# Second-layer messages of a two-layer graph network added up in three tables by turns in place of four

## The chip, the cores and the metric

One core of one Trainium2 chip runs the whole kernel as one program. The time is the device time of one execution in microseconds (us). The engines named below: TensorE (PE, with its weight loads as PEld), VectorE (DVE), ScalarE (ACT), GpSimd (POOL), and SyncE (SP), which issues most of the transfers.

## The reference

Two message-passing layers over a graph with N = 12500 nodes of 160 numbers (64 scalars and 32 vectors of three) and E = 212500 edges, sorted by `dst`. The second layer, which the change touches, gathers by `dst` and sums by `src` (`edge_index` is `src, dst`; inside the layer the first is the one that is summed over):

```python
h = jnp.maximum(_layernorm(x, axis=-1), 0.0)
# second layer: s, v are linear maps of h; sh1 = unit vector of edge_attr_3 times sqrt(3)
w = jax.nn.relu(edge_feature @ W_fc1) @ W_fc2
xs = s[dst]
xv = v[dst]
out0a = w0 * xs
out0b = w3 * (jnp.einsum('emi,ei->em', xv, sh1) * INV_SQRT3)
out1a = (w1 * xs)[:, :, None] * sh1[:, None, :]
out1b = w2[:, :, None] * xv
out1c = w4[:, :, None] * (jnp.cross(xv, sh1[:, None, :]) * INV_SQRT2)
tp = jnp.concatenate([out0a, out0b, out1a.reshape(E, -1), out1b.reshape(E, -1), out1c.reshape(E, -1)], axis=-1)
agg = jax.ops.segment_sum(tp, src, num_segments=N) / DENOM
out_s = agg[:, :96] @ W_out_s + skip_s
out_v = jnp.einsum('nmi,mk->nki', agg[:, 96:].reshape(N, 128, 3), W_out_v) + skip_v
# a gate on out_s and out_v, and x + that is the output
```

So each edge gives a message of 480 numbers, and the messages of all edges with the same `src` are added into one row of a table with one row per node. The sum doesn't depend on how the edges are split over partial tables, up to rounding.

## The kernel before

Edges are padded to T = 1668 tiles of P = 128. Everything runs from one unrolled program, in stages.

**First layer** (lines 362 to 401). For each of 556 groups of three tiles, GpSimd gathers source rows with an indirect DMA per tile (line 367), and the sums are formed by matmuls and written by SP. In the same stage SP clears the tables of the second layer, three blocks of 128 rows at a time (`clear(acc1[k], C1, b0, 3)`, line 395, the DMA itself at line 185), once in four groups until all K tables of 99 blocks are cleared: 33 clears a table. VectorE also finds here, for every tile, which edge is the first with its `src`, and leaves in `where` the row to which each edge's sum goes: the first of equal edges gets the node's row, the others a trash row.

**Node stage** between the layers (lines 480 to 509): writes the gather table `ft1` and the skip term `skip`.

**Second layer** (lines 583 to 714). The loop runs over 417 groups `q` of G = 4 tiles. For each group VectorE builds `same` (which edges of a tile share a `src`, line 565) and the messages (`second_messages`, lines 535 to 560). `scattered` then handles each tile `j`: a matmul adds equal edges within the tile into `sm` in PSUM (line 671), ScalarE copies it to `o` in SBUF (line 673), and GpSimd issues an indirect DMA that adds the 128 rows of 480 floats (1920 bytes) to rows `where` of a table in HBM (line 675). The tile `o` has eight buffers (line 672), so a copy waits until the scatter eight tiles earlier has landed. Tile `t = q*G + j` goes to table `t % K`. Two scatters into one table may add into the same row, so the framework makes each wait until the previous one into its table has landed. POOL has nothing else to do in this stage. Every 12 tiles, SP loads the next inputs (`rows`, 384 KB; `ft`, 384 KB; `to` and `fw`, four each of 24 and 20 KB), one (`rows`) or two turns of 12 tiles ahead.

**Final stage** (lines 729 to 758). 49 turns over pairs of node blocks (FB = 2). `added` loads the two blocks from each of the K tables into `t` (named `sums`, line 738) and the skip term (line 740), and adds the tables on VectorE (lines 742 and 743); it is called one turn ahead of `mapped`, and `t` has four buffers. `mapped` transposes on TensorE (lines 408, 409), copies (411 on ScalarE, 412 on VectorE), multiplies (416, 417), and VectorE adds the skip term (line 754); `second_out` applies the gate (lines 719 to 724) and ScalarE's queue stores the result. VectorE's instructions are kept in the order in which the program writes them: both adds of the next pair, then for each block of this pair the copy of line 412 and the add of line 754, then the gate of the pair before.

Of the kernel before, what the change touches and what calls it, by code (L numbers as in the profile page):

```python
# [14 lines left out]
ALU = mybir.AluOpType  # L15
# [26 lines left out]
NCH = T // CT  # L42
CE = CT * P
CW = CT // S
K = 4
TR = NP
NT = NP + P
C0 = 385
# [6 lines left out]
def gnn_kernel(ctx: ExitStack, tc: tile.TileContext, a, out):  # L55
    nc = tc.nc
    tt = nc.vector.tensor_tensor
# [82 lines left out]
    for m in range(3):  # L140
        f0 = m * 96
        while f0 < (m + 1) * 96:
            k, p0 = divmod(f0, P)
# [36 lines left out]
    sums = [dram.tile([NT, 4 * HC], F32, name=f"sums_{k}") for k in range(2)]  # L180
    acc1 = [dram.tile([NT, C1], F32, name=f"acc1_{k}") for k in range(K)]
    skip = dram.tile([NP, 192], F32, name="skip")

    def clear(t, cols, b0=0, n=NT // P):
        nc.sync.dma_start(t.rearrange("(p b) c -> p b c", p=P)[:, b0:b0 + n, :],
                          zero[:, None, :cols].to_broadcast([P, n, cols]))
# [112 lines left out]
    def keep(i):  # L299
        tc.keep_in_program_order(i)  # L300
# [15 lines left out]
    with ExitStack() as st:  # L316
# [45 lines left out]
        for gr in range(NG):  # L362
# [30 lines left out]
            k, b0 = divmod(gr // CW * 3, NT // P)  # L393
            if gr % CW == 1 and k < K:
                clear(acc1[k], C1, b0, 3)
# [7 lines left out]
    def mapped(wk, ps, s, nv, wv, ws, v0=0, keep=lambda i: i):  # L403

        s0 = 0 if v0 else 3 * nv
        tp = ps.tile([P, 4, P], F32, name="tp")
        for m in range(3):
            nc.tensor.transpose(tp[:nv, m, :], s[:, v0 + m * nv:v0 + (m + 1) * nv], ident)
        nc.tensor.transpose(tp[:96, 3, :], s[:, s0:s0 + 96], ident)
        st = wk.tile([P, 4, P], F32, name="st")  # L410
        nc.scalar.copy(st[:nv, 0:3], tp[:nv, 0:3])
        keep(nc.vector.tensor_copy(st[:96, 3], tp[:96, 3]))
        n = 96 + ws.shape[1]
        y = ps.tile([P, n], F32, name="y")
        for m in range(3):
            nc.tensor.matmul(y[:, m * V1:(m + 1) * V1], st[:nv, m, :], wv, start=True, stop=True)
        nc.tensor.matmul(y[:, 96:n], st[:96, 3, :], ws, start=True, stop=True)
        return y
# [61 lines left out]
    with tc.tile_pool(name="nwk1", bufs=2) as wk, tc.tile_pool(name="nps1", bufs=2, space=PSUM) as ps:  # L480
        for c in range(NCB):
            rows = []
            for k in range(2):
                t = wk.tile([P, CB, 4 * HC], F32, name="rows", bufs=3)
# [99 lines left out]
    with ExitStack() as st:  # L584
# [84 lines left out]
        def scattered(q, j, same, msg):  # L669
# [5 lines left out]
            nc.gpsimd.indirect_dma_start(  # L675
                out=acc1[t % K][:, :], out_offset=bass.IndirectOffsetOnAxis(ap=where[:, t:t + 1], axis=0),
                in_=o, in_offset=None, compute_op=ALU.add)
# [17 lines left out]
        for q in range(NQ1):  # L695
            ch, k = divmod(q, CT // G)
# [19 lines left out]
    def second_out(wk, s, xs, n, keep=lambda i: i):  # L716

        sig = wk.tile([P, n, 96], F32, name="sig")
        nc.scalar.activation(sig, s[:, :, 96:192], AF.Sigmoid)
        keep(tt(s[:, :, 96:160], s[:, :, 96:160], sig[:, :, 0:64], ALU.mult))  # L720
        keep(tt(split(s[:, :, 0:96]), split(s[:, :, 0:96]), sig[:, :, None, 64:96].to_broadcast([P, n, 3, V1]), ALU.mult))
        y = wk.tile([P, n, D], F32, name="yo")
        keep(tt(y[:, :, :S0], xs[:, :, :S0], s[:, :, 96:160], ALU.add))
        keep(tt(planes(y[:, :, S0:]), planes(xs[:, :, S0:]), split(s[:, :, 0:96]), ALU.add))
        return y
# [3 lines left out]
    with tc.tile_pool(name="fwk", bufs=4) as wk, tc.tile_pool(name="fps", bufs=3, space=PSUM) as ps:  # L729
        def two(t, b0):  # L730
            return t[0:NP, :].rearrange("(p b) c -> p b c", b=NB)[:, b0:b0 + FB, :]

        def added(b0):
            if b0 >= NB:
                return
            t = wk.tile([P, K, FB, C1], F32, name="sums")
            for k in range(K):
                nc.sync.dma_start(t[:, k], two(acc1[k], b0))
            s = wk.tile([P, FB, 192], F32, name="s")
            nc.sync.dma_start(s, two(skip, b0))  # L740
            h = K // 2
            keep(tt(t[:, 0:h], t[:, 0:h], t[:, h:K], ALU.add))
            keep(tt(t[:, 0], t[:, 0], t[:, 1], ALU.add))
            return t, s


        ready, gated = added(0), None
        for b0 in range(0, NB + FB, FB):
            t, s = ready or (None, None)
            ready = added(b0 + FB)  # L750
            if t is not None:
                for b in range(FB):
                    y = mapped(wk, ps, t[:, 0, b, :], 128, o1_v, o1_s, 96, keep)
                    keep(tt(s[:, b, :], y, s[:, b, :], ALU.add))
            if gated:
                y = second_out(wk, gated[0], xr[:, gated[1]:gated[1] + FB, :], FB, keep)
                nc.scalar.dma_start(two(out, gated[1]), y)
            gated = (s, b0)
# [37 lines left out]
    with tc.If(flag > 0):  # L796
        with tc.tile_pool(name="gwk", bufs=1) as wk, tc.tile_pool(name="gps", bufs=1, space=PSUM) as ps:
# [14 lines left out]
            with tc.For_i(0, NQ) as q:  # L812
# [4 lines left out]
                for a_ in range(2):  # L817
# [4 lines left out]
                    for j in range(S):  # L822
                        t = a_ * S + j
# [43 lines left out]
            with tc.For_i(0, T // G) as q:  # L867
# [10 lines left out]
                for j in range(G):  # L878
                    h, c = divmod(j, 2)
# [67 lines left out]
```

## Time and profile before

| what | us |
|---|---|
| three runs | 6560.95, 6565.19 (median), 6582.53 |
| the profiled execution, its own time | 6562.27 |
| its span, first to last instruction | 6560.5 |
| first layer's gathers, first to last issue | 280.8 to 2425.8 |
| clears of the second layer's tables | 282.9 to 1108.5 |
| second layer's scatters, first to last issue | 2864.5 to 6160.7 |
| final stage, first load of a table to the last | 6167.1 to 6530.6 |
| busy: PE, DVE, POOL, ACT | 5848.0, 4708.9, 4260.3, 2430.5 |

Half of the time is the scatter loop of the second layer. Shares of busy time for the whole span mix stages with different limits (PE 89%, DVE 72%, POOL 65%), so each stage is looked at by itself: its steps, and what each engine waited for. In rows of groups the columns are line, engine, operation, what is written from what, count, then busy time and mean ns of one, then the engine's idle time just before and what ended most of it. In rows of the timeline they are start, duration, engine, line, operation, and in brackets the idle time before and its releaser. In rows of waits: engine, tile and line that waited, for what, total us, times, longest. In rows of windows: the stretch, its length, then busy time and count of each engine asked for, the granted clock of TensorE, the share of the DMA engines and GB/s.

### The profile page before, as it was taken

How to read it: one execution, taken by the hardware profiler on the slowest of the kernel's cores; microseconds unless marked ns; L12 is line 12 of the kernel's file. 1: busy time of each engine (PE TensorE's matmuls, PEld its weight loads, DVE VectorE, ACT ScalarE, POOL GpSimd, SP SyncE). 2: the span in 40 equal slices, each digit the busy share in tenths (PEclk: the TensorE clock that was granted, in tenths of full speed). 3: DMA queues.
4: the chain of work that ended last, by engine and by line, in shares of the span. 5: the costliest groups of instructions: out<-in, count | busy, mean ns of one | idle time of the engine just before them, and what ended most of it. 6: DMA issues, size and time to landing. Idle time of an engine off the chain costs nothing.

```text
span 6560.5 us, 87170 instructions
## 1 busy us (share of the span) xinstructions
PE 5848.0 (89%) x22974; PEld 3347.0 (51%) x22974; DVE 4708.9 (72%) x11396; ACT 2430.5 (37%) x7896; POOL 4260.3 (65%) x3346
## 2 busy tenths in 40 slices
PE   6899999999999988869999999999999999999676
PEld 4566656566666556634444444444444444444466
DVE  5587878777865547667777777777777777777566
ACT  2222222222222213334555555555555555555311
POOL 0277777777777760047787877777787777878400
PEclk9999999999999998879999999999999999999755
DMA  9687887554544347469999999999999999999987
GB/s 351 242 252 239 246 243 223 126 127 126 126 110 93 92 118 278 186 126 165 166 165 166 166 165 165 166 167 166 166 167 165 167 165 164 168 164 167 215 303 262
DMA packets 653194, 1186.35 MB, mean 181 GB/s; under 512 B 94385, under 2 KB 506225, under 8 KB 648978
## 3 DMA queue, kind: packets, MB, share of 16 engines
q0 software_dynamic: 320256, 546.78, 53.4%
q1 hardware_dynamic: 319954, 617.36, 29.2%
q10 hardware_dynamic: 12480, 16.56, 0.7%
q8 instruction: 185, 3.03, 0.2%
q14 instruction: 319, 2.61, 0.1%
HBM read 528.25 MB, written 652.09 MB: 180 GB/s over the span
## 4 chain that ended last, share of the span: by engine, by line


## 5 line engine op out<-in xcount | busy, mean ns | idle before, releaser
L675 POOL DMA_INDIRECT acc<-o,where x1668 | 2621.4, 1572 | 1114.1 <-ACT o L673 695.8
L367 POOL DMA_INDIRECT g<-ft,idx_src x1668 | 1637.7, 982 | 787.3 <-issue 683.6
L671 PE MATMUL sm<-msg,same 128*128 128x480 f32 x3336 | 1842.2, 635 | 58.6 <-ACT o L673 54.0
L673 ACT COPY o<-sm 128x480 f32<-128x480 f32 x1668 | 931.5, 558 | 1502.5 <-DMA acc<-o,where 1053.6
L339 PE MATMUL ag<-pr,fac 128*128 128x320 f32 x3336 | 1084.0, 462 | 100.3 <-DVE pr L288 98.6
L657 PEld LDWEIGHTS gs<-fw,pick 32*128 32x128 f32 x3336 | 484.0, 188 | 797.7 <-ACT xv L533 436.8
L657 PE MATMUL gs<-fw,pick 32*128 32x160 f32 x3336 | 691.1, 327 | 196.3 <-ACT xv L533 195.4
L565 DVE TENSOR_TENSOR same<-rows,wp 128x512 f32<-128x512 int16 x417 | 286.6, 687 | 745.5 <-ACT wp L666 570.3
L671 PEld LDWEIGHTS sm<-msg,same 128*128 128x128 f32 x3336 | 544.6, 196 | 450.9 <-issue 219.3
L339 PEld LDWEIGHTS ag<-pr,fac 128*128 128x128 f32 x3336 | 604.4, 194 | 309.4 <-DVE pr L288 112.3
L294 PE MATMUL wp<-w,hs 64*128 64x192 f32 x3336 | 701.5, 345 | 0.6 <-ACT hs L358 0.6
L287 DVE TENSOR_TENSOR pr<-wp,g 128x384 f32<-128x384 f32 x556 | 309.4, 556 | 516.1 <-DMA g<-ft,idx_src 430.2
L294 PEld LDWEIGHTS wp<-w,hs 64*128 64x128 f32 x3336 | 536.3, 190 | 254.8 <-issue 253.0
L342 ACT COPY so<-ag 128x161 f32<-128x161 f32 x556 | 164.4, 296 | 1269.0 <-PE ag L339 1269.0
L538 DVE TENSOR_TENSOR pp<-xv,wp 128x1152 f32<-128x1152 f32 x417 | 561.7, 1347 | 0.0
L640 PE MATMUL wp<-w,hs 64*128 64x224 f32 x3336 | 552.8, 409 | 0.0
L389 DVE SCALAR_TENSOR_TENSOR seen<-rows,srcf,before 128x128 f32<-128x128 int16 x1668 | 523.4, 347 | 1.5 <-DMA rows<-in_src_low 1.5
L640 PEld LDWEIGHTS wp<-w,hs 64*128 64x128 f32 x3336 | 257.9, 189 | 397.3 <-issue 397.1
L288 DVE TENSOR_TENSOR pr<-wp,g 128x576 f32<-128x576 f32 x556 | 415.5, 747 | 0.0
L538 DVE TENSOR_TENSOR msg<-wp,xv 128x768 f32<-128x768 f32 x417 | 399.4, 958 | 14.3
L538 DVE TENSOR_TENSOR msg<-msg,wp 128x768 f32<-128x768 f32 x417 | 397.9, 954 | 14.5
L374 DVE TENSOR_TENSOR fac<-hit,sh 128x384 f32<-128x384 bf16 x556 | 309.5, 557 | 66.9 <-PE ag L339 53.3
(146 smaller groups left out, 6335.4 us busy)
## 6 DMA issues: line engine op xcount, KB each, us to landing
rows<-in_src_low SPq DMA_DIRECT2D x278, 384.0 KB
acc<-zero SPq DMA_DIRECT2D x132, 720.0 KB
sums<-acc SPq DMA_DIRECT2D x196, 480.0 KB
sums<-zero SPq DMA_DIRECT2D x2, 31878.0 KB
rows<-sums SPq DMA_DIRECT2D x28, 2254.0 KB
ft<-in_ea SPq DMA_DIRECT2D x139, 384.0 KB
sums<-so SPq DMA_DIRECT2D x556, 80.5 KB
g<-ft,idx_src POOLq DMA_INDIRECT x1668
```

The costliest lines, as they stand in the source:

```text
L288: tt(o[:, :, :, S0:].rearrange("p t k (m u) -> p t k m u", m=3), w[:, :, :, None, S0:96].to_broadcast([P, n, 2, 3, V1]), split(g[:, :, S0: ...
L294: keep(nc.tensor.matmul(wp[:, j].rearrange("p (k u) -> p k u", k=2)[:, :, 0:96], hs[a_ * 64:(a_ + 1) * 64, j * P:(j + 1) * P], w0_2[a_ * 6 ...
L339: keep(nc.tensor.matmul(ag[:, 0:2 * HB], fac[:, j].rearrange("p m w -> p (m w)"), pr[:, j, :], start=j == 0, stop=j == S - 1))
L367: nc.gpsimd.indirect_dma_start(out=g[:, j, :], out_offset=None, in_=ft0[:, :], in_offset=bass.IndirectOffsetOnAxis(ap=idx["src"][:, t0 + j ...
L374: tt(fac, hit[:, :, None, :].to_broadcast([P, S, 4, W]), sh[:, t0:t0 + S, :, None].to_broadcast([P, S, 4, W]), ALU.mult)
L389: nc.vector.scalar_tensor_tensor(seen, hidden["rows"][:, u * P:(u + 1) * P], srcf[:, t0 + j:t0 + j + 1], before, op0=ALU.is_equal, op1=ALU ...
L538: keep(tt(*args))
L640: keep(nc.tensor.matmul(part["wp", q][:, 2 * h + c, :224], part["hs", q][h * 64:(h + 1) * 64, c * P:(c + 1) * P], w1_2[h * 64:(h + 1) * 64 ...
L657: keep(nc.tensor.matmul(gs[:, j - lo, :], part["pick", ch][u * W:(u + 1) * W, v, :], part["fw", ch][u * W:(u + 1) * W, :], start=True, sto ...
L671: keep(nc.tensor.matmul(sm, same[:, j, :], msg[:, j, S0:], start=True, stop=True))
L673: keep(nc.scalar.copy(o, sm))
L675: nc.gpsimd.indirect_dma_start(out=acc1[t % K][:, :], out_offset=bass.IndirectOffsetOnAxis(ap=where[:, t:t + 1], axis=0), in_=o, in_offset ...
```

## The change

The second layer's sums are kept in three tables, tile `t` going to table `t % 3`. One table fewer is cleared in the first layer and loaded in the final stage. There, two adds of 128x960 (the second and the third table, one after the other, into the first) stand in place of one of 128x1920 (two tables onto two) and one of 128x960.

```diff
@@ -42,7 +42,7 @@
 CW = CT // S
-K = 4
+K = 3
 TR = NP
@@ -738,9 +738,8 @@
                 nc.sync.dma_start(t[:, k], two(acc1[k], b0))
             s = wk.tile([P, FB, 192], F32, name="s")
             nc.sync.dma_start(s, two(skip, b0))
-            h = K // 2
-            keep(tt(t[:, 0:h], t[:, 0:h], t[:, h:K], ALU.add))
-            keep(tt(t[:, 0], t[:, 0], t[:, 1], ALU.add))
+            for k in range(1, K):
+                keep(tt(t[:, 0], t[:, 0], t[:, k], ALU.add))
             return t, s
```

## The prediction

> **What bounds the kernel now.** I read the page's costliest groups first. The largest is the scatter of line 675: GpSimd issues one indirect DMA for each of the 1668 tiles of the second layer.
>
> ```profile
> L675 POOL DMA_INDIRECT acc<-o,where x1668 | 2621.4, 1572 | 1114.1 <-ACT o L673 695.8
> L673 ACT COPY o<-sm 128x480 f32<-128x480 f32 x1668 | 931.5, 558 | 1502.5 <-DMA acc<-o,where 1053.6
> ```
>
> The first row is POOL at 1.572 us a scatter, the second ScalarE standing 1053.6 us until scatters have landed. The instructions of line 675 start at 2864.5 us (first) and 6160.7 us (last): 3296.2 us, so 1667 steps of 1.977 us. Then the timeline in the middle of this stage:
>
> ```profile
> 4002.89 1.55 POOL L675 DMA_INDIRECT acc<-o,where  x1 [0.30 <-issue]
> ...
> 4004.74 1.55 POOL L675 DMA_INDIRECT acc<-o,where  x1 [0.30 <-issue]
> ...
> 4006.60 1.55 POOL L675 DMA_INDIRECT acc<-o,where  x1 [0.30 <-issue]
> ...
> 4008.46 1.55 POOL L675 DMA_INDIRECT acc<-o,where  x1 [0.31 <-ACT o L673]
> ...
> 4011.10 0.56 ACT L673 COPY o<-sm 128x480 f32<-128x480 f32 x1 [2.17 <-DMA acc<-o,where]
> ...
> 4011.75 1.55 POOL L675 DMA_INDIRECT acc<-o,where  x1 [1.73 <-ACT o L673]
> ```
>
> Back to back, scatters start 1.858 us apart (1.553 + 0.305), as 78% of all steps do. The step to 4011.75 took 3.29. The releaser printed there misleads: copies run four ahead of POOL (by their order, each copy ends a median 8.7 us before its own scatter starts), so the copy at 4011.10 is not what POOL waited for. Both waited for the scatter issued at 4002.89. ScalarE needs that scatter's buffer (eight of `o`, and its copy is four ahead); POOL needs its table, four scatters back. The completion records put that landing at 4011.02, which is 8.13 us after the issue, and POOL starts 0.73 us after it. So the rule of this stage is: a scatter starts at the later of 1.858 us after its predecessor and 0.73 us after the landing of the last one in its table. Taking every landing from the completion records, the rule gives the starts to within 0.33 us in 98 of 100.
>
> The latency, issue to last completion, over 1661 complete records: 5% under 5.13 us, a quarter under 5.52, median 5.86, mean 6.15, a quarter over 6.77, 5% over 7.77. It follows the loads that come with every 12 tiles: its mean is 5.6 to 5.8 for the fourth to ninth scatter of twelve, and 6.46, 7.54, 7.16, 6.54 for the tenth to the next first. With four tables a landing is late only above 4 x 1.858 - 0.73 = 6.70 us, about a quarter of them; that and 134 long POOL instructions (1.82 us) make 1.977 out of 1.858.
>
> The rest of the stage hides behind this:
>
> ```profile
> POOL acc L675 <- ACT o L673: 253.3, 367, 2.3
> POOL acc L675 <- issue: 195.9, 636, 1.3
> POOL acc L675 <- DMA acc<-o,where: 114.2, 351, 1.7
> ...
> ACT o L673 <- DMA acc<-o,where: 1037.5, 818, 4.2
> ```
>
> These are the waits between 2900 and 6100 us: what held ScalarE longest there is POOL's landings, not its own inputs.
>
> **The change, part by part.**
>
> *Three tables in the scatter loop.* Nothing is added to any engine; every wait of POOL at line 675 moves from the scatter four back to the one three back. In time that leaves 3 x 1.858 - 0.73 = 4.85 us for the landing instead of 6.70. Only 1.4% of the recorded landings are that early, so POOL would wait nearly every time, and the step becomes (latency + 0.73) / 3. Nothing is queued behind a scatter on POOL but the next scatter; ScalarE, with its eight buffers, then stops four ahead as it does now, and PE and DVE behind it. The price of three under way is not in this trace; bounds are its latencies. Upper: the mean as it stands, 6.15, gives 6.88 / 3 = 2.293. Lower: if the bursts vanished, 5.65 gives 2.127. The nearest row is the scatters issued while exactly two others were still under way, just what the new loop has: 780 of them, mean 6.10. In the quiet part (fourth to ninth) those 551 have a median of 5.62 and those with three under way 5.63, so fewer in flight doesn't shorten it; a longer step lets each burst of loads meet somewhat fewer scatters. I take 6.05: 6.78 / 3 = 2.26, times 1667 is 3767, which is +471 us (bounds +250 and +526).
>
> The Trainium skill, "DMA: Bandwidth & Descriptors", section "Anatomy of one DMA — SWDGE (gpsimd) path", speaks against a loss: a DMA issued from GpSimd takes about 2.0 us plus its bytes at 436 GB/s. For 128 rows of 1920 B that estimate is 2.56 us, under the 4.85 us allowed; by it the loop would keep its time. The median of 5.86 in this trace, for a transfer that also reads and adds, decides against it.
>
> *Final stage, adds.* Before, the timeline of DVE in one of 49 turns:
>
> ```profile
> 6302.46 2.14 DVE L742 TENSOR_TENSOR sums<-sums 128x1920 f32<-128x1920 f32 x1
> 6304.64 1.16 DVE L743 TENSOR_TENSOR sums<-sums 128x960 f32<-128x960 f32 x1
> 6305.71 0.28 DVE L412 COPY st<-tp 96x128 f32<-96x128 f32 x1
> 6307.16 0.36 DVE L754 TENSOR_TENSOR s<-y,s 128x192 f32<-128x192 f32 x1 [1.17 <-PE y L417]
> ```
>
> From the first add to the copy behind it is 3.25 us. The change makes two adds of the 128x960 form: 1.16 + 0.04 to the second (the gap between these two rows), and 1.07 from it to the copy: 2.27. The 0.98 saved is on the path: DVE runs without a break but for two waits for PE, and PE's transposes wait for line 743. 49 x 0.98 = 48 us less. Bounds: 0 if PE's part, at a granted clock of 0.50 here, took it all; 54 if the waits shrink too.
>
> *Final stage, loads.* 196 loads of 480 KB become 147. DVE waits for one only at the start (first load issued 6167.12, first add 6174.57); a quarter of 7.4 us is the most this gives: -1, between 0 and -2. Were DVE ever to wait for loads, the 24.1 MB less (49 x 480 KB) at the 303 GB/s of 6250 to 6350 us would be 80 us; it doesn't.
>
> *First layer, clears.* 33 clears of 720 KB fall away, issued by SP between 283 and 1108 us. POOL's gathers cover them, in windows with clears and without:
>
> ```profile
> 300.00:1100.00 800.00, 610.34 (x623) 0.98 0.81 245
> 1200.00:2000.00 800.00, 610.10 (x624) 0.97 0.49 122
> ```
>
> Line 367 makes 623 gathers in 800 us with the clears and 624 without: nothing gained. Without that cover, 24.3 MB at 245 GB/s would be 99 us.
>
> **Sum.** 471 - 48 - 1 = +422, on a span of 6560.5: 6982.5, and 1.8 us lie around the span in that execution (6562.3): 6984, say 6985. The profiled execution is 2.9 us under the median of the runs shown, 6565.2.
>
> **Rivals.**
>
> *One late landing holds all three tables.* POOL issues in order, so a scatter delayed by a burst delays the two behind it by all but the slack, and delays don't average. Speaks for it: in the new loop the slack between the step and the 1.858 floor is only 0.4 us, against a burst of 1.9 us (7.54 - 5.65) and quiet latencies that run from 5.3 to 6.2 us, 10% to 90%. Against: the burst's own extra, summed over scatters (6 us) and divided by three, is already in my mean. If it holds, the step is 2.30 to 2.36: +538 to +638, less 49, or 7050 to 7150.
>
> *The latency shrinks with the load* (the faster side). The share of the DMA engines is 1.03 in the two windows of the loop (2900 to 4500 and 4500 to 6100 us), so the engines could be the bound, and fewer scatters under way would only shorten the queue. The first two scatters, alone, landed in 4.76 and 4.69 us. Decides from a mean latency under 5.29: then 3 x (1.977 + 0.029) covers landing and 0.73, and the final stage's 49 us tip it. At 5.0 the step is 1.91: 1667 x 0.067 = -112, with -49 about 6400. Against it: where a backlog is drained, landings follow each other in 1.2 us, so the engines aren't full at 1.98, and the quiet latencies above don't fall with one fewer under way.
>
> *The change doesn't do what it says:* the wait that counts is that for the eight buffers of `o`, not the tables. Then the loop keeps 1.977 and the final stage gives 6513. Against: the semaphore that POOL waits on ahead of line 675 is that of the scatter four back.
>
> **Chances and range.** Forecast 0.77, late landings 0.13, shrinking latency 0.06, no effect 0.04. The forecast's time is that of its own case, and the range runs from a mean latency of 5.72 (2.15 a step, 6800) to a step of 2.335 into the first rival (7110); outside lie the two faster cases and some 0.04 at each end. A difference within 0.3%, 20 us, is no change that a measurement can tell: 0.02, the edge of the shrinking latency; faster 0.08; slower 0.90.
>
> **What would show it.** Steps at line 675 mostly between 1.9 and 2.8 us, few at 1.858, the last scatter near 6630 us; POOL's idle time before line 675 near 1580 us; in the final stage two 128x960 adds a turn and a turn some 1 us shorter; line 367 unchanged. Wrong if scatters still start 1.858 us apart for most, if latencies recorded have a mean under 5.3 us, or if the turn of the final stage stays at its length.

## The result and the profile after

Three tables take 7138.5 us (median of four runs, 7122.8 to 7159.6) against 6565.7 before: 1.087 times as long, 95% interval 1.083 to 1.091. Slower, as forecast, but above the range of 6800 to 7110. The profiled execution took 7159.6 us with a span of 7157.7, so 597.2 us more span than before; it is the longest of the four, 21 us above their median.

Where the 597.2 us are, by the starts of the scatters in the two traces:

| stretch | before | after | difference | forecast |
|---|---|---|---|---|
| start to the first scatter | 2864.5 | 2868.3 | +3.9 | 0 |
| first to last scatter | 3296.2 | 3908.7 | +612.4 | +471 |
| last scatter to the end | 399.8 | 380.7 | -19.1 | -49 |

The two costliest groups of the second layer after, as shown of before:

```profile
L675 POOL DMA_INDIRECT acc<-o,where x1668 | 2602.5, 1560 | 1746.2 <-ACT o L673 1447.4
L673 ACT COPY o<-sm 128x480 f32<-128x480 f32 x1668 | 932.0, 559 | 2064.5 <-DMA acc<-o,where 1567.2
```

POOL is as busy as before and stands 632 us longer. The releaser ACT is again the coincidence told of in the prediction: a copy and a scatter are freed by the same landing, and each copy ends a median 11.9 us before its own scatter starts. The waits of the loop say it from ScalarE's side (2900 to 6600 us):

```profile
ACT o L673 <- DMA acc<-o,where: 1499.5, 889, 4.6
POOL acc L675 <- ACT o L673: 971.2, 910, 3.5
```

What the forecast had missed is in the timeline of POOL alone:

```profile
4021.13 1.55 POOL L675 DMA_INDIRECT acc<-o,where  x1 [0.60 <-ACT o L673]
4023.33 1.55 POOL L675 DMA_INDIRECT acc<-o,where  x1 [0.65 <-ACT o L673]
4025.77 1.55 POOL L675 DMA_INDIRECT acc<-o,where  x1 [0.89 <-ACT o L673]
4029.60 1.55 POOL L675 DMA_INDIRECT acc<-o,where  x1 [2.28 <-ACT o L673]
4031.45 1.55 POOL L675 DMA_INDIRECT acc<-o,where  x1 [0.30 <-issue]
4033.31 1.55 POOL L675 DMA_INDIRECT acc<-o,where  x1 [0.31 <-issue]
4035.74 1.55 POOL L675 DMA_INDIRECT acc<-o,where  x1 [0.87 <-ACT o L673]
```

By the completion records, the scatter of 4021.13 landed at 4028.86, after 7.74 us; SP had issued a load of `rows` while it was under way:

```profile
4022.64 0.35 SPq L602 DMA_DIRECT2D rows<-in_src_low  x1
```

POOL started the next into its table 0.73 later, at 4029.60. The two behind it had their tables earlier: that of 4031.45 could have started 0.36 us sooner, that of 4033.31 1.01 us sooner. They stand behind the late one on POOL and follow at 1.858. Over the whole loop 49% of the steps are at 1.858, where the forecast had expected few; 276 of the 1667 are over 3.0 us.

That can be summed up in one account. From a scatter to the next into the same table, one lap of three steps, pass its latency, 0.73 us, and the time for which the table is free and POOL is not: 5.96 + 0.73 + 0.344 = 7.03 us on the mean, which is three steps of 2.345. The mean latency forecast was 6.05. The 0.344, "lost" below, is what the forecast left out: 1667 x 0.344 / 3 = 191 us.

### The profile page after: what moved, and what is told of

The parts are those of the page before. It is cut to its first block, busy times and chain, and to the rows that moved or that the text cites. A ratio compares the mean times of both kernels' runs of the same rounds, so it can differ in the third digit from the quotient of the medians.

```text
span 7157.7 us, 87114 instructions
## 1 busy us (share of the span) xinstructions
PE 6075.6 (85%) x22974; PEld 3474.2 (49%) x22974; DVE 4657.4 (65%) x11396; ACT 2434.1 (34%) x7896; POOL 4243.5 (59%) x3346
## 4 chain that ended last, share of the span: by engine, by line
## 5 line engine op out<-in xcount | busy, mean ns | idle before, releaser
L671 PE MATMUL sm<-msg,same 128*128 128x480 f32 x3336 | 1965.8, 674 | 85.0 <-ACT o L673 73.0
L657 PE MATMUL gs<-fw,pick 32*128 32x160 f32 x3336 | 744.2, 346 | 553.1 <-ACT xv L533 552.4
L657 PEld LDWEIGHTS gs<-fw,pick 32*128 32x128 f32 x3336 | 523.0, 202 | 1162.8 <-ACT xv L533 778.4
L671 PEld LDWEIGHTS sm<-msg,same 128*128 128x128 f32 x3336 | 595.3, 211 | 499.1 <-ACT o L673 250.8
L630 PE MATMUL hp<-ft,w 128*128 128x256 f32 x834 | 315.2, 467 | 54.5 <-DMA fw<-ft 53.1
```

The lines of the kernel that those rows point to most:

```text
L630: keep(nc.tensor.matmul(hp, w1_1, part["ft", ch][:, k * 2 * P:(k + 1) * 2 * P], start=True, stop=True))
L657: keep(nc.tensor.matmul(gs[:, j - lo, :], part["pick", ch][u * W:(u + 1) * W, v, :], part["fw", ch][u * W:(u + 1) * W, :], start=True, sto ...
L671: keep(nc.tensor.matmul(sm, same[:, j, :], msg[:, j, S0:], start=True, stop=True))
```

## The experiments

Theory A: the lost time comes from the bursts of loads, since one late landing holds back the scatters behind it on POOL. Theory B: three ordered scatters lose it against the 1.858 floor anyway. Theory C: the DMA engines are full, and set the step. The stages are compared by their traces. Kernels ran on different chips, and on one of them (k3_double_loads, k2, k4_pe, k5_pe) the kernel before took 7200.9 us, because what comes ahead of the second layer's scatters is slower there (first scatter of k4_pe at 3502.6 us, 2864.5 in the kernel before on the other chip); ratios are to the kernel before on the same chip.

| run | tables | loop, us | step | mean latency | lost a lap | last scatter to end |
|---|---|---|---|---|---|---|
| before | 4 | 3296.2 | 1.977 | 6.15 | - | 399.8 |
| after | 3 | 3908.7 | 2.345 | 5.96 | 0.344 | 380.7 |
| k3_no_loads | 3 | 3448.6 | 2.069 | 5.35 | 0.121 | 380.5 |
| k3_spread | 3 | 3767.1 | 2.260 | 5.82 | 0.229 | 381.8 |
| k4_no_loads | 4 | 3118.8 | 1.871 | 5.37 | - | 400.2 |
| k5 | 5 | 3122.4 | 1.873 | 6.34 | - | 444.0 |
| k3_pe_order | 3 | 3900.9 | 2.340 | 5.96 | 0.335 | 329.2 |

**Loads left out, three tables (k3_no_loads).** From the third turn of 12 tiles on, the loaded inputs of the first two are used again, so the messages are not those of their edges; the rows that the scatters add to stay the same.

```diff
-            if ch < NCH:
+            if 2 <= ch < NCH:
+                part["rows", ch] = part["rows", ch - 2]
+            elif ch < NCH:
                 part["rows", ch] = ld.tile([P, CE], I16, name="rows")
...
         def loads(ch):
             if ch >= NCH:
+                return
+            if ch >= 2:
+                for n in ("ft", "to", "fw"):
+                    part[n, ch] = part[n, ch - 2]
                 return
             ft = ld.tile([P, CT // 2 * P], F32, name="ft")
```

> Three tables; in the second layer the inputs of the first two turns of 12 tiles are used again for all later ones, so the bursts of loads (rows, ft, to, fw) are left out; the scatters and their rows are the same. Theory A (the bursts delay one scatter, POOL issues in order, so the two behind it are held though their tables are free, and each lap of three loses 0.34 us more than its latency): latencies even out near 5.2 us, the lost 0.34 falls under 0.1, step near (5.2 + 0.73) / 3 = 1.98 us, the loop near 3300 us in place of 3909. Theory B (the 0.34 is the play of three ordered scatters against the 1.858 floor, bursts or not): latency 5.2 as well, but the 0.34 stays, step near 2.09, loop near 3485. Theory C (the DMA engines are full and set the step): the step falls only by the loads' share of the engines, some 15%, to about 2.0, with POOL starting long after the landing.

Measured: 6698.3 us, ratio 1.020 (1.018 to 1.022); loop 3448.6. The timeline of POOL near the same time:

```profile
4010.19 1.55 POOL L681 DMA_INDIRECT acc<-o,where  x1 [0.56 <-ACT o L679]
4012.05 1.55 POOL L681 DMA_INDIRECT acc<-o,where  x1 [0.30 <-ACT o L679]
4014.16 1.55 POOL L681 DMA_INDIRECT acc<-o,where  x1 [0.56 <-ACT o L679]
4016.16 1.55 POOL L681 DMA_INDIRECT acc<-o,where  x1 [0.44 <-ACT o L679]
4018.32 1.55 POOL L681 DMA_INDIRECT acc<-o,where  x1 [0.61 <-ACT o L679]
4020.32 1.55 POOL L681 DMA_INDIRECT acc<-o,where  x1 [0.45 <-ACT o L679]
4022.18 1.56 POOL L681 DMA_INDIRECT acc<-o,where  x1 [0.30 <-ACT o L679]
4024.11 1.55 POOL L681 DMA_INDIRECT acc<-o,where  x1 [0.37 <-issue]
4026.39 1.57 POOL L681 DMA_INDIRECT acc<-o,where  x1 [0.72 <-ACT o L679]
4029.53 1.56 POOL L681 DMA_INDIRECT acc<-o,where  x1 [1.57 <-ACT o L679]
```

Long steps have become rare: most of these lie between 1.86 and 2.28, one is 3.14, and in the whole loop 31 are over 3.0 us in place of 276. The lost time falls to 0.121 a lap: two thirds of it came with the loads, and a third stays without them, as theory B had meant. Latency fell less than expected (5.35, not 5.2), so the loop is nearer to B's number than to A's, though it is the latency that puts it there. C falls as the whole account: it had POOL start long after the landing, and here too most starts that waited come 0.73 us after it.

**Loads left out, four tables (k4_no_loads).** The same edit in the kernel before.

> The kernel before, four tables, with the second layer's loads left out as in k3_no_loads (inputs of the first two turns of 12 tiles used again). Theory A: latencies even near 5.4 us, all under the 6.70 us that four tables allow, so every step is at POOL's floor: 1.86 to 1.88, loop 3100 to 3135 us. The change then costs 3449 - 3115 = some 330 us without the loads and 612 with them. If something else than landings made 1.977 out of 1.858, the loop stays near 3296.

Measured: 6381.0 us, ratio 0.973 (0.971 to 0.975).

```profile
L681 POOL DMA_INDIRECT acc<-o,where x1668 | 2604.5, 1561 | 951.2 <-ACT o L679 461.8 <-DMA acc<-o,where 276.2 <-issue 164.6
```

Busy 2604.5 and idle 951.2, of which 1667 x 0.305 = 508 is the fixed gap and nearly all of the rest one wait ahead of the first scatter (435.4 us): POOL runs at its floor, 94% of the steps. So the loads cost four tables 177 us and three tables 460 us, and of the 612 us that the change costs in the loop, 330 remain without them (3448.6 - 3118.8).

**Loads in thirds (k3_spread).** `rows` and `ft` are loaded in three parts, one for each group of four tiles; the bytes are the same.

```diff
...
+            sources(ch + 1, k)
+            features(ch + 2, k)
             if k == 0:
-                sources(ch + 1)
                 loads(ch + 2)
```

> Three tables; the same bytes of rows and ft are loaded in three thirds, one for each group of 4 tiles, in place of one load for every 12 tiles. Theory A: latencies keep about their mean (5.8 to 6.0 us) but their peaks (7.2 and 7.8 us) fall, the time lost beyond latency falls from 0.34 to about 0.1 a lap, step about 2.2 us, total 6890 to 6950 us. Theory B: 0.34 stays, total 7080 to 7140.

Measured: 7017.7 us, ratio 1.069 (1.067 to 1.070): between the two. The parts helped less than meant, because peaks of the mean latency remain at the third scatter of twelve (6.5 us, 7.2 before the split) and at the tenth and eleventh (7.0 and 7.1, were 7.8 and 7.2). With flatter peaks the lost time fell too, 0.344 to 0.229.

**Loads twice (k3_double_loads).** `rows` and `ft` are each loaded a second time into a tile that nothing reads.

```diff
-                nc.sync.dma_start(part["rows", ch], a["src_low"][:, ch * CE:(ch + 1) * CE].to_broadcast([P, CE]))
+                again = ld.tile([P, CE], I16, name="again", bufs=1)
+                for t in (part["rows", ch], again):
+                    nc.sync.dma_start(t, a["src_low"][:, ch * CE:(ch + 1) * CE].to_broadcast([P, CE]))
...
```

> Three tables; rows and ft of the second layer are each loaded a second time into tiles that nothing reads, so the bursts are twice as long. Theory A (bursts, with POOL issuing in order): the time lost beyond latency grows again, from 0.12 a lap without loads and 0.34 with them to between 0.45 and 0.7; mean latency 6.3 to 6.6 us, step 2.5 to 2.65, total 7400 to 7640 us. Theory B (play against the floor, bursts or not): it stays near 0.34, step near 2.47, total near 7350.

Measured: 7905.2 us, ratio 1.098 (1.095 to 1.100) on the slower chip, which makes the expected totals useless; its loop is 4029.8, a step of 2.417, below both expectations. Too many completion records are missing in that trace (819 of 1668 scatters lack at least one of their 16) to tell latency from lost time. So twice the loads cost 121 us more, where the first dose cost 460; how that splits stays open, and A's claim that longer bursts lose more is not shown.

**Two tables (k2).**

```diff
-K = 3
+K = 2
```

> Two tables. A scatter waits for the landing two back; 2 x 1.858 - 0.73 = 2.99 us are allowed, which no recorded landing meets. Theory A: two ordered scatters have 2.2 us of room between the floor and a lap of near 6.1 us, about as much as a burst adds, so nearly nothing is lost beyond latency (under 0.1 a lap against 0.34 with three): step = (5.2 to 5.5 + 0.73) / 2 = 2.97 to 3.15 us, loop 4950 to 5250 us, total 8150 to 8450. Theory B': whenever the wait binds, 0.3 is lost a lap: step 3.12 to 3.3. If the step went with something else than landings (tables, bytes), it would not follow latency over two.

Measured: 8574.0 us, ratio 1.191 (1.188 to 1.193) on the same chip as the run above. The loop is 4753.2, a step of 2.851, under the expected range. Only 6% of the steps are at the floor, so a lap is nearly latency + 0.73 alone, and latency at most 2 x 2.851 - 0.73 = 4.97 (the 1379 complete records have a mean of 4.89): lower than I had thought with two under way, and the mechanism, landing over the number of tables, holds.

**Five tables (k5).** `K = 5`, and the clears twice as often, so that all are clear in time.

```diff
-K = 3
+K = 5
...
-            k, b0 = divmod(gr // CW * 3, NT // P)
-            if gr % CW == 1 and k < K:
+            k, b0 = divmod(gr // 2 * 3, NT // P)
+            if gr % 2 == 1 and k < K:
```

> Five tables (cleared twice as often in the first layer, so that all are clear in time; five loads and four adds of 128x960 a turn in the final stage). Waits are for the landing five back, 5 x 1.858 - 0.73 = 8.56 us allowed. Theories A and B: nearly no landing is late, step 1.87 to 1.89 us, loop about 3130 us (3296 with four); final stage some 50 us longer; total about 6450 us. Theory C: engines are full at 1.977 already, the loop stays near 3296 and the total is near 6610.

Measured: 6431.7 us, ratio 0.979 (0.977 to 0.981): some 2% faster than the kernel before, and so faster than both. 92% of the steps are at the floor, with the loads in place and a higher latency than before, 6.34 us; C is out, since the engines take a scatter every 1.873 us beside the loads. The loop gives 174 us and the final stage takes 44 of them back. A window of that stage:

```profile
6050.00:6400.00 350.00, 227.93 (x966) 196.24 (x966) 269.16 (x484) 52.93 (x121) 0.00 (x0) 0.50 0.93 328
```

The share of the DMA engines is 0.93 at 328 GB/s, yet DVE waits there little for loads and more for PE:

```profile
DVE s L753 <- PE y L417: 66.7, 80, 0.8
DVE sums L742 <- DMA sums<-acc: 10.2, 14, 1.9
```

The clears, 33 more than before, cost nothing: the first scatter starts at 2865.4 us.

**PE's order in the final stage (k3_pe_order, k4_pe, k5_pe).** The transposes of both blocks of a pair are made first and then the products, in that written order. VectorE's two copies out of the transposes move ahead with them (`turned_over`), so its order changes too, and the runs don't separate the two.

```diff
...
+                sts = [turned_over(t[:, 0, b, :]) for b in range(FB)]
                 for b in range(FB):
-                    y = mapped(wk, ps, t[:, 0, b, :], 128, o1_v, o1_s, 96, keep)
+                    y = ps.tile([P, 192], F32, name="y")
+                    for m in range(3):
+                        keep(nc.tensor.matmul(y[:, m * V1:(m + 1) * V1], sts[b][:, m, :], o1_v, start=True, stop=True))
+                    keep(nc.tensor.matmul(y[:, 96:], sts[b][:96, 3, :], o1_s, start=True, stop=True))
                     keep(tt(s[:, b, :], y, s[:, b, :], ALU.add))
```

> Three tables; in the final stage PE's instructions are kept in an order written out: the transposes of both blocks of a pair, then its products, so that none stands behind a transpose of the next pair, which waits for the adds. If PE's order is what held the final stage's turns at 7.41 us (forecast: 6.74 on the mean, from 7.72), turns fall to 6.0 to 6.6 us and the total by 40 to 65 us, to about 7085. If PE's own work at a granted clock of 0.5 sets the turn, it stays at 7.4 and the total at 7138.

> The kernel before, four tables, with the written-out PE order in the final stage. With the order held the same as in k3_pe_order (turn 6.35 us), the turn shows what the fourth table costs by itself: 7.33 us if the 0.98 us of adds lies on the path, 6.4 to 6.6 if it hides behind PE, 7.0 to 7.3 if the loads (2.33 MB a turn at some 320 to 335 GB/s) become the bound. Total 6500 to 6545 us.

> Five tables and the written-out PE order. The scatter loop stays near 3122 us. If the loads bound the final stage of five tables (2.82 MB in 8.41 us are 335 GB/s), the turn stays at 8.4 us and the total near 6430; if PE's order does, as with three, the turn falls to 7.3 to 7.8 us and the total to 6380 to 6405.

Measured with three tables: 7088.5 us, ratio 1.079 (1.076 to 1.081), 50 us under the change, and turns of 6.35 us. With four: ratio 0.998 (0.997 to 0.999), turns of 7.35. With five: ratio 0.981 (0.978 to 0.983), turns of 8.73, no gain over 8.42 of k5 (medians). Loads are not the reason: from 6680 to 7030 us of k5_pe, DVE waits 1.1 us for loads and 79.3 us for PE. From the first add to the copy are 4.64 us there and 3.26 in k4_pe, which is the whole 1.38 us between 8.73 and 7.35; and k5's own order has DVE wait for PE 0.83 us twice a turn, less than the 0.64 and 1.35 of the written one. The timeline of DVE, first of the changed kernel, then of k3_pe_order:

```profile
6903.99 2.33 DVE L742 TENSOR_TENSOR sums<-sums 128x960 f32<-128x960 f32 x2
6906.23 0.28 DVE L412 COPY st<-tp 96x128 f32<-96x128 f32 x1
6907.69 0.36 DVE L753 TENSOR_TENSOR s<-y,s 128x192 f32<-128x192 f32 x1 [1.17 <-PE y L417]
6907.96 0.28 DVE L412 COPY st<-tp 96x128 f32<-96x128 f32 x1
6910.12 0.36 DVE L753 TENSOR_TENSOR s<-y,s 128x192 f32<-128x192 f32 x1 [1.88 <-PE y L417]
```

```profile
6906.30 2.35 DVE L742 TENSOR_TENSOR sums<-sums 128x960 f32<-128x960 f32 x2
6908.56 0.48 DVE L753 COPY st<-tp 96x128 f32<-96x128 f32 x2
6909.68 0.36 DVE L767 TENSOR_TENSOR s<-y,s 128x192 f32<-128x192 f32 x1 [0.64 <-PE y L766]
6911.38 0.36 DVE L767 TENSOR_TENSOR s<-y,s 128x192 f32<-128x192 f32 x1 [1.35 <-PE y L766]
```

From the first add to the copy are 2.24 and 2.26 us in both, as forecast (2.27). The waits for PE are 1.17 and 1.88 us in the changed kernel, the same as in the turn shown of before, and 0.64 and 1.35 with the other order.

**Thirds and PE's order, four tables (k4_spread_pe).**

> Four tables, rows and ft loaded in thirds, and the written-out PE order. Theory A: latencies peak near 7.0 in place of 7.5 us against the 6.70 allowed, step 1.91 to 1.94 us, loop 3185 to 3235 (3296 before); final stage some 18 us shorter as in k4_pe; total 60 to 125 us under the kernel before of the same chip.

Measured: 6478.5 us, ratio 0.988 (0.986 to 0.990), loop 3231.8 and 382.1 to the end, as expected. Like k5, it beats both kernels, here by 1.2% and at the number of tables of before.

## Why the prediction was wrong

**The step of the loop** is the one that failed: "the step becomes (latency + 0.73) / 3". It averages, as if each table were a loop of its own. The two prices in it were right: the latency 5.96 us against 6.05, and 0.73 from landing to start (0.730 to 0.732 for most late starts, before and after). By them the step is 2.23; it was 2.345, since POOL issues in order and a scatter that is late holds those behind it, while an early landing (15% come within the 4.85 us that three steps at the floor allow) gains nothing. The loop came out 141 us above the forecast: 191 us lost, less 50 because the latency was 0.09 us shorter than taken. The account can be checked on the records of the changed kernel alone: starts worked out from each recorded latency, 0.73 and the 1.858 floor sum to 3884 us (3909 measured); with every latency set to their mean they sum to 3717. In this account the 167 us between are the price of unevenness, and k3_no_loads shows most of its source: with the loads gone the lost time falls from 0.344 to 0.121 a lap. (The 25 us that the account is short lie mostly in 63 starts that come 1.04 to 2.02 us after a landing instead of 0.73; why is open.) The same latencies in a shuffled order sum to some 4050, so it is their spread that costs, and not that the late ones come in a row.

The trace of before already gave nearly this: its own recorded latencies, put through the same rule with three tables, sum to 3948 us, within 1% of the 3909 measured, where the prediction's mean gave 3767. For four tables the prediction went by the late tail (a quarter over 6.70 us); for three it went by the mean.

**The first rival was right.** Its step of 2.30 to 2.36 holds the 2.345, and its 7050 to 7150 us the time. I had given it 0.13 because "the burst's own extra, summed over scatters (6 us) and divided by three, is already in my mean". That is the error: a late landing also delays the scatters behind it, as the 0.36 and 1.01 us above show, and the mean holds none of that.

**The final stage, adds.** The saving of 0.98 us a turn was right for one and the same order on PE: 8.41 us before, 7.41 after; 7.35 with four tables and 6.35 with three in the written order. But the turn shown before was one of two kinds. Turns of 8.41 and 7.03 us alternated, 7.72 on the mean, as the framework had ordered PE differently in every second one. The turn just ahead of the one shown waits for PE 0.83 and 0.84 us, not 1.17 and 1.88:

```profile
6299.80 0.36 DVE L754 TENSOR_TENSOR s<-y,s 128x192 f32<-128x192 f32 x1 [0.83 <-PE y L417]
6300.08 0.28 DVE L412 COPY st<-tp 96x128 f32<-96x128 f32 x1
6301.19 0.36 DVE L754 TENSOR_TENSOR s<-y,s 128x192 f32<-128x192 f32 x1 [0.84 <-PE y L417]
```

In the changed kernel all turns have the longer kind, 7.41. So 0.31 a turn is left, 15 us of 48. This term was mis-sized because one turn stood for all; two in a row would have shown it.

**The rest.** The clears cost nothing, as forecast: line 367 makes 622 gathers in the first 800 us window and 621 in the second, 623 and 624 before. The start of the final stage gave 2.1 us (first load to first add 5.4 us, 7.4 before), where 1 was taken. The 2.9 us between the profiled execution of before and its median was no part of the error; the profiled execution after lies 21 us above its median, which leaves some 573 us by medians for the 597 by traces.

**The other rivals.** *The latency shrinks with the load:* it does, 6.34, 6.15 and 5.96 us with five, four and three tables and 4.89 with two, but with three not under the 5.29 from which it would have decided. Landings over 6.70 us are 26% with four tables and with three; what shrinks is the quick side, a tenth of them under 5.30 us before and under 4.75 after. The prediction's "fewer in flight doesn't shorten it" compared two others under way with three. In the changed kernel 133 scatters started with one other under way and landed in 5.09 us on the mean, 1462 with two in 6.04; whether the one fewer or the end of a burst does it, no run separates. *No effect:* out; k4_no_loads, k5 and k2 each follow the tables. The estimate of 2.56 us from the Trainium skill ("DMA: Bandwidth & Descriptors", "Anatomy of one DMA — SWDGE (gpsimd) path") is met by no scatter here: the fastest of before took 4.60 us, the fastest of all runs 4.42.

## What to carry to other kernels

Where n transfers in a ring are issued by one engine in order, the step is not the mean latency over n, which is too short where latencies are uneven. Work it out start by start, as the later of the engine's floor and the landing n back, with the latencies as they are recorded, since a late one also holds back those behind it and an early one is lost at the floor. The slack that counts is that against the latency at its peaks, so ask what else loads the queues when they come; here one table more bought 8.56 us of room and the floor, at 44 us in the final stage. And look at several turns of a stage before one is priced, because a framework's order may alternate.

## What the runs showed of the hardware

A scatter that adds 128 rows of 1920 bytes takes 5.4 us on the mean from its start to its last landing without any loads (k3_no_loads and k4_no_loads, two or three others under way), 3.8 us beyond its 1.55 us on POOL; with two tables, so with one other under way, it takes 4.9 us beside the loads. From the landing to the next start POOL needs 0.73 us at the median in every kernel in which it waited.

One chip ran the same first layer at three quarters of the pace, and no run shows why: in the window from 300 to 1100 us its k4_pe made 478 gathers at a granted clock of 0.83, and the kernel before on another chip 623 at 0.98, while the scatter loop took 3306.9 and 3296.2 us. So a time from one of these chips is no measure for a kernel run on the other; the stages tell which part differs.
